# Two graph layers on one core: layer 1's norm statistics move to ScalarE, long tiles get a fifth pair of rows, four transposes move back, and the unused pass stores through SyncE

## The chip, the cores and the metric

The kernel runs on one core of a Trainium2 chip. The metric is the device time of one execution in microseconds (us); less is better. TensorE is called PE in the profile, VectorE is DVE, ScalarE is ACT, GpSimd is POOL and SyncE is SP. Every engine works through its own instructions in order and waits on semaphores for the others.

## The reference, cut to what matters

There are 3327 nodes with 512 features and one sparse adjacency matrix. Layer 0 is a graph attention layer, layer 1 a gated mix of attention and plain sum. Each is followed by a residual and a layer norm. Layer 1, which the change touches, is:

```python
def _L1_gnn_ref(x, adj_a, adj_b, W_sa, a_sa, W_gcnb, b_gcnb, Wa, ba, Wb, bb):
    attn_a = sigmoid(concatenate([adj_a @ x, x], axis=1) @ Wa.T + ba)
    attn_b = sigmoid(concatenate([adj_b @ x, x], axis=1) @ Wb.T + bb)
    h = x @ W_sa
    scores = (h @ a_sa[0, :Hd])[:, None] + (h @ a_sa[0, Hd:])[None, :]
    e = where(adj_a != 0, exp(-leaky_relu(scores, 0.01)), 0.0)
    x_a = (e / (sum(e, axis=1, keepdims=True) + 1e-05)) @ h
    x_b = adj_b @ (x @ W_gcnb) + b_gcnb
    return sigmoid(attn_a * x_a + attn_b * x_b)
x = _layernorm(x + _L1_gnn_ref(x, adj, adj, ...))     # both adjacencies are the same
```

The layer norm takes the mean and the variance of each node's 512 numbers. The inputs are about as sparse as 9 neighbours to a node.

## The kernel before

**Two passes.** `sparse_pass` does all the work as long as no node has more neighbours than its tables hold; it computes a flag for that. `dense_pass` stands in an `If` on the flag and isn't taken with these inputs. At the end of the program every engine loads the flag and takes the other side of the branch, whose few instructions bring the semaphores to the values that they would have after `dense_pass`.

**Nodes and tiles.** Nodes are sorted by their number of neighbours and cut into 26 tiles of 128. `CAPS` gives the number of neighbour rows of each tile, from 4 to 14. Two tiles of 14 have an extra "stair" row for the few nodes with still more. Rows are fetched from a table in memory by indirect DMAs that GpSimd issues (`gather`, L615), one DMA for a row of each of 128 nodes. They land in seven buffers of six rows, three tiles ahead of their use.

**Layer 1's loop.** The last loop runs over 26 tiles and three more turns to empty the pipeline. The order of tiles alternates long and short ones; the first five have 5, 6, 6, 6 and 7 rows and the last two 5 and 4. In turn i, tile j is summed, the next tile j1 gets its weights, the one before, jp, is projected, and jpp, two before, is finished. Order on each engine is the order of the calls, for the scheduler is off (`manual_schedule`). In short:

- ScalarE scales jp's plain sum (`sp`, L1027); TensorE turns `sw` and then `sp` of jp, four 128x128 transposes each (`turn`, L998), and ScalarE copies both out (`sT`, L1000).
- TensorE adds tile j's unpaired rows into `acc` (`plain_sum(j, False)`, L988).
- VectorE adds each row, weighted, into `sw` (`weighted`, L967), and adds pairs of rows in place (L969), so that TensorE sums one row for two. `paired` says which: four pairs a tile, five from 13 rows on.
- VectorE makes `za` of jpp from the projection (L1035) and ScalarE takes its tanh (L1037).
- TensorE projects jp's `sw` (`project`, `po<-wsa`, L1007), adds the sums of two (L988), and projects jp's `sp` (`po<-wg`, L1007). VectorE makes tile j1's weights in between (`weights_a`, L902 to L924).
- VectorE adds the residual to jpp's `za` (L1059), finishes j1's weights (`weights_b`, L929 to L932). ScalarE then starts the next weighted sum with the tile's own row (`scaled_first`, `sw`, L951). VectorE takes the statistics of `za` (`norm.add`: `bn_stats` L660 and `bn_aggr` L661). At the ends of eight groups of up to four tiles, 13 small instructions follow (`rsqrt`, L669 to L676).
- In the next turn ScalarE normalises the group's tiles (L1052) and GpSimd scatters them to the output (L145).

The next turn's `weighted` begins with `sw`, which ScalarE has just started (L951).

Of the kernel before, what the change touches and what calls it, by code (L numbers as in the profile page):

```python
# [8 lines left out]
F32 = mybir.dt.float32  # L9
AF = mybir.ActivationFunctionType  # L10
ALU = mybir.AluOpType
# [3 lines left out]
P = 128  # L15
LN_EPS = 1e-5
I32 = mybir.dt.int32
BF16 = mybir.dt.bfloat16
# [7 lines left out]
CAPS = (14, 12, 11, 10, 9, 9, 8, 8, 7, 6, 6, 5) + (14, 13, 11, 10, 10, 9, 9, 8, 8, 7, 7, 6, 5, 4)  # L26
# [10 lines left out]
GRP = 4  # L37
# [42 lines left out]
def sparse_pass(  # L80
# [39 lines left out]
    nc = tc.nc  # L120
    N, F = out.shape
# [33 lines left out]
    x1 = [x1a.tile([P, NG[0], ROW], F32, name="x1a"), None]  # L155
# [19 lines left out]
    def place(j):  # L175

        return (0, j) if j < NG[0] else (1, j - NG[0])
# [5 lines left out]
    def row1(j):  # L183
        g, i = place(j)
        return x1[g][:, i, :]
# [403 lines left out]
    m0 = ctx.enter_context(tc.tile_pool(name="m0", bufs=2))  # L589
# [89 lines left out]
    class Norm:  # L679
# [6 lines left out]
        def add(self, k, y):  # L686
# [8 lines left out]
            self.first, self.mv = k + 1, None  # L695
            return done


    first = list(range(NG[0]))

# [123 lines left out]
    norm = Norm(m0, "n0", {3, 7, 11, 15, 19, 22, 24, 25})  # L824
    weigh_a(order0[0])
    weigh_b(order0[0])
    ready = [[], []]
    for i in range(NT + 3):
        if i + AHEAD < NT:
            j = order0[i + AHEAD]  # L830
# [3 lines left out]
        ready = [ready[1], []]  # L834
# [4 lines left out]
        if 0 < i <= NT:  # L839
            j = order0[i - 1]  # L840
            y = row1(j)[:, 0:F]
# [3 lines left out]
            done = norm.add(i - 1, y)  # L845
# [24 lines left out]
    m1 = ctx.enter_context(tc.tile_pool(name="m1", bufs=2))  # L870
# [65 lines left out]

    def paired(j):

        left = 4 + (CAPS[j] >= 13)
        got_ = set()  # L940
        for s0, n, g, _ in got[j]:
            for i in range(0, n - 1, 2):
                if left:
                    got_.add(s0 + i)
                    left -= 1
        return got_

    def scaled_first(j):

        sw = sums[j] = m1.tile([P, F], F32, tag="sw", name=f"sw{j}")  # L950
        nc.scalar.activation(sw, row1(j)[:, 0:F], AF.Copy, scale=ew[j][:, 0:1])  # L951
        if j in T0:
            scaled = m1.tile([P, F], F32, tag="scaled", name=f"scaled{j}", bufs=1)
            nc.scalar.activation(scaled, stair[j][:, 0:F], AF.Copy, scale=ws2[j])
            stair_sum[j] = ps1.tile([P, F], F32, tag="stair", name=f"stair_sum{j}")
            nc.tensor.matmul(stair_sum[j], to_node, scaled, start=True, stop=True)

    def weighted(j, part):

        e, sw, two = ew[j], sums[j], paired(j)  # L960
        cut = max(two) + 2
        for s0, n, g, _ in got[j]:
            for i in range(n):
                s = s0 + i
                if (s < cut) != (part == 0):
                    continue
                nc.vector.scalar_tensor_tensor(sw, g[:, i, 0:F], e[:, s : s + 1], sw, ALU.mult, ALU.add)  # L967
                if s - 1 in two:
                    nc.vector.tensor_add(g[:, i, 0:F], g[:, i - 1, 0:F], g[:, i, 0:F])  # L969
        if part == 1 and j in T0:  # L970
            nc.vector.tensor_add(sw, stair_sum[j], sw)

    def plain_sum(j, sums_of_two):
        two = paired(j)
        single, double = [(ident, row1(j)[:, 0:F])], []
        for s0, n, g, _ in got[j]:
            for i in range(n):
                if s0 + i - 1 in two:
                    double.append((ident, g[:, i, 0:F]))
                elif s0 + i not in two:  # L980
                    single.append((ident, g[:, i, 0:F]))
        if j in T0:
            single.append((to_node, stair[j][:, 0:F]))
        if not sums_of_two:
            plain[j] = ps.tile([P, F], F32, tag="acc", name=f"acc1_{j}", bufs=2)
        rows = double if sums_of_two else single
        for i, (to, row) in enumerate(rows):
            nc.tensor.matmul(  # L988
                plain[j], to, row, start=(not sums_of_two and i == 0),
                stop=(sums_of_two and i == len(rows) - 1),  # L990
            )

    def turn(j, half):

        src = sums[j] if half == 0 else zs[j, "sp"]
        pt = (ps, ps1)[half].tile([P, KT, P], F32, tag="pt", name=f"pt{half}_{j}")
        for k in range(KT):
            nc.tensor.transpose(pt[:, k, :], src[:, k * P : (k + 1) * P], ident)  # L998
        sT = zs[j, half] = m1.tile([P, KT, P], F32, tag=f"sT{half}", name=f"sT{half}_{j}")
        nc.scalar.copy(sT, pt)  # L1000

    def project(j, half):
        sT, wt = zs[j, half], (wsa, wg)[half]
        if half == 0:
            proj[j] = ps1.tile([P, F], F32, tag="po", name=f"po{j}", bufs=2)
        for k in range(KT):
            nc.tensor.matmul(proj[j], sT[:, k, :], wt[:, k, :], start=(half + k == 0), stop=(half + k == KT))  # L1007

    ends = {3, 7, 11, 15, 19, 22, 24, 25}
    norm = Norm(m1, "n1", ends)  # L1010
    at_ = lambda i: order[i] if 0 <= i < NT else None
    for i in range(3):
        got[at_(i)] = gather(table1, at_(i))
# [1 line left out]
    weights_a(at_(0))  # L1015
    weights_b(at_(0))
    scaled_first(at_(0))
    ready = None
    for i in range(NT + 3):
        j, j1, jp, jpp = at_(i), at_(i + 1), at_(i - 1), at_(i - 2)  # L1020
        if at_(i + 3) is not None:
            got[at_(i + 3)] = gather(table1, at_(i + 3))
        if j1 is not None:
            own_score(j1)
        if jp is not None:
            sp = zs[jp, "sp"] = m1.tile([P, F], F32, tag="sp", name=f"sp{jp}")
            nc.scalar.activation(sp, plain[jp], AF.Copy, scale=gates[jp][:, 1:2])  # L1027
            turn(jp, 0)
            turn(jp, 1)
        if j is not None:  # L1030
            plain_sum(j, False)
            weighted(j, 0)
        if jpp is not None:
            za = zs[jpp] = m1.tile([P, F], F32, tag="za", name=f"za{jpp}", bufs=GRP + 3)
            nc.vector.scalar_tensor_tensor(za, bias_g, gates[jpp][:, 1:2], proj[jpp], ALU.mult, ALU.add)  # L1035

            nc.scalar.activation(za, za, AF.Tanh, scale=0.5)  # L1037
        if jp is not None:
            project(jp, 0)
        if j is not None:  # L1040
            plain_sum(j, True)
        if j1 is not None:
            weights_a(j1)
        if j is not None:
            weighted(j, 1)
        if jp is not None:
            project(jp, 1)
        if ready:
            k0, scale, shift = ready
            for k in range(k0, i - 2):  # L1050
                z = zs[order[k]]
                nc.scalar.activation(  # L1052
                    z, z, AF.Identity, scale=scale[:, k - k0 : k - k0 + 1], bias=shift[:, k - k0 : k - k0 + 1]
                )
                scatter("out", out, own(order[k]), z, N - 1)
            ready = None
        if jpp is not None:
            za = zs[jpp]
            nc.vector.scalar_tensor_tensor(za, za, 0.5, row1(jpp)[:, 0:F], ALU.mult, ALU.add)  # L1059
        if j1 is not None:  # L1060
            weights_b(j1)
            scaled_first(j1)
        if jpp is not None:
            ready = norm.add(i - 2, zs[jpp])


@with_exitstack
def dense_pass(
# [21 lines left out]
    nc = tc.nc  # L1090
    N, F = x.shape
    H, _, FO = W0.shape
# [45 lines left out]
    x1 = x1_pool.tile([P, NT, F], F32, name="x1")  # L1138
# [25 lines left out]
    with tc.tile_pool(name="feats", bufs=1) as feats_pool:  # L1164
# [3 lines left out]
        with tc.tile_pool(name="p0", bufs=1) as p0, tc.tile_pool(name="p0s", bufs=2) as p0s, tc.tile_pool(  # L1168
            name="p0ps", bufs=2, space=PSUM
# [15 lines left out]
            for c0 in range(0, N, CH):  # L1185
# [3 lines left out]
                for t in range(c0 // P, (c0 + cw + P - 1) // P):  # L1189
                    r, o = rows(t), t * P - c0  # L1190
# [45 lines left out]
        with tc.tile_pool(name="m0", bufs=2) as m0p, tc.tile_pool(name="m0o", bufs=1, space=PSUM) as pso, tc.tile_pool(  # L1236
            name="m0t", bufs=2, space=PSUM
        ) as pst:
            for n0 in range(0, N, NB):
                nw = min(NB, N - n0)  # L1240
                tiles = list(range(n0 // P, (n0 + nw + P - 1) // P))
                rr = m0p.tile([P, 2, H, NB], F32, tag="rr", name=f"rr{n0}")
                for j, t in enumerate(tiles):
                    r = rows(t)
# [7 lines left out]
                for t0, g in groups(G):  # L1252
# [4 lines left out]
                    for t in range(t0, t0 + g):  # L1257
                        r = rows(t)
# [30 lines left out]
                for j, t in enumerate(tiles):  # L1289
                    r = rows(t)  # L1290
# [9 lines left out]
                    y = x1[:r, t, :]  # L1300
# [21 lines left out]
    with tc.tile_pool(name="p1", bufs=1) as p1, tc.tile_pool(name="p1s", bufs=2) as p1s, tc.tile_pool(  # L1322
        name="p1ps", bufs=2, space=PSUM
# [18 lines left out]
        for t in range(NT):  # L1342
            r = rows(t)
# [24 lines left out]
    with tc.tile_pool(name="m1", bufs=2) as m1p, tc.tile_pool(name="m1o", bufs=1, space=PSUM) as pso, tc.tile_pool(  # L1368
        name="m1t", bufs=2, space=PSUM
    ) as pst:  # L1370
        for n0 in range(0, N, NB):
# [3 lines left out]
            for j, t in enumerate(tiles):  # L1375
                r = rows(t)
# [36 lines left out]
            for j, t in enumerate(tiles):  # L1413
                r = rows(t)
# [13 lines left out]
                za = m1p.tile([P, F], F32, tag="za", name=f"za{t}")  # L1428
# [5 lines left out]
                y = x1[:r, t, :]  # L1434
# [4 lines left out]
            normalise(m1p, f"b{n0}", tiles, stats)  # L1439
            for t in tiles:  # L1440
                r = rows(t)
                nc.gpsimd.dma_start(out[t * P : t * P + r, :], x1[:r, t, :])


def gat_then_gated_gnn(tc, x, xT, xB, xL, adj, adjT, adjB, adjL, diag, xo, W0, W0B, b0, a_self, a_neigh, *rest):
# [71 lines left out]
```

## Time and profile before

| | us |
|---|---|
| median of 3 runs | 974.06 (973.56 to 977.38) |
| profiled execution | 1108.9 |
| its span | 1107.2 |
| layer 1's loop in it, first gather wait to last scatter | about 659 to 1095 |
| PE, DVE, ACT, POOL busy in the span | 830.1, 716.9, 278.9, 623.3 |

The profiled execution took 134.8 us longer than the median, so durations in it show which engine waits for which, and a sum of differences is made in its microseconds. A row of the groups gives the line, the engine, the operation, output and input, the count, and then the busy time, the mean duration of one in ns and the idle time before it. A row of the timeline gives the start, the duration, and in brackets how long the engine had been idle and what ended that. Successive instructions overlap a little, so the distance from start to start is what an instruction costs its engine.

### The profile page before, as it was taken

To read this page: it belongs to the slowest core of one execution; us is meant where nothing else is said; L and a number is where in the kernel's file an instruction comes from. 1 tells how busy PE (TensorE), PEld (TensorE's weight loads), DVE (VectorE), ACT (ScalarE), POOL (GpSimd) and SP (SyncE) were. 2 spreads that over 40 slices of the span, in tenths; PEclk is the share of its full clock that TensorE was granted. 3 is DMA by queue.
4 is the path that set the end of the run, shared out by engine and by line. 5 is a ranking of instruction groups with operands and counts; after the bars stand their busy time and mean duration, and the time that the engine had idled before them with its cause. 6 is when DMAs were issued, how large, how long until landed. Compare 5 with 4: busy or idle time off the path is not lost.

```text
span 1107.2 us, 10091 instructions
## 1 busy us (share of the span) xinstructions
PE 830.1 (75%) x2534; PEld 435.9 (39%) x2534; DVE 716.9 (65%) x2118; ACT 278.9 (25%) x820; POOL 623.3 (56%) x664
## 2 busy tenths in 40 slices
PE   4499973028768697868848976689898989697992
PEld 3377751014334343434424432244344434343441
DVE  4286786187333673855536655398797989968872
ACT  1022120004221442433313421122222222131331
POOL 7410247607675466466766437737777777776311
PEclk9698995557778898989979985889898999898997
DMA  9899899603976567486766417726676576766200
GB/s 324 316 359 399 346 321 381 198 0 105 394 232 173 149 204 206 147 307 197 213 187 202 145 62 200 204 77 190 178 191 185 173 193 174 189 177 180 76 29 31
DMA packets 74243, 221.88 MB, mean 200 GB/s; under 512 B 14944, under 2 KB 19216, under 8 KB 73280
## 3 DMA queue, kind: packets, MB, share of 16 engines
q0 software_dynamic: 47008, 153.87, 47.1%
q1 hardware_dynamic: 24512, 65.17, 15.6%
q10 hardware_dynamic: 2656, 2.10, 0.6%
q8 instruction: 23, 0.38, 0.1%
q14 instruction: 44, 0.36, 0.1%
HBM read 200.01 MB, written 28.55 MB: 206 GB/s over the span
## 4 chain that ended last, share of the span: by engine, by line
PE 40%; issue 16%; POOL 12%; DVE 12%; another core or an unknown queue 9%; DMA 5%; ACT 5%; ACTq 0%; DVEq 0%; POOLq 0%; SPq 0%
PE acc L763 12%; PE pf L351 7%; POOL g L615 7%; PE po L1007 6%; PE acc L988 6%; PE pcol L787 2%; DMA g<-table,srt 2%; DMA at<-in_adjB 2%; PE acc L752 2%; DVE sw L967 2%; POOL out L145 1%; ACT g L758 1%; POOL lists L145 1%; PE pt L998 1%
## 5 line engine op out<-in xcount | busy, mean ns | idle before, releaser
L615 POOL DMA_INDIRECT g<-table,srt x464 | 476.1, 1026 | 217.9 <-issue 145.8
L763 PE MATMUL acc<-g,ident 128*128 128x512 f32 x504 | 238.3, 629 | 2.4 <-issue 2.4
L967 DVE SCALAR_TENSOR_TENSOR sw<-g,e,sw 128x512 f32<-128x512 f32 x226 | 169.4, 750 | 13.5 <-ACT sw L951 6.2
L763 PEld LDWEIGHTS acc<-g,ident 128*128 128x128 f32 x504 | 103.5, 206 | 139.8 <-issue 126.8
L988 PE MATMUL acc<-g,ident 128*128 128x512 f32 x262 | 126.4, 617 | 13.5 <-DMA g<-table,srt 9.5
L1007 PE MATMUL po<-wsa,sT 128*128 128x512 f32 x208 | 101.4, 633 | 18.3 <-issue 13.3
L351 PE MATMUL pf<-w,xc 128*128 128x260 f32 x416 | 103.4, 411 | 13.4 <-DVE w L291 13.4
L760 DVE TENSOR_TENSOR g<-g,w 128x512 f32<-128x512 f32 x176 | 109.7, 692 | 0.6
L351 PEld LDWEIGHTS pf<-w,xc 128*128 128x128 f32 x416 | 84.7, 206 | 29.4 <-DVE w L291 13.9
L1007 PE MATMUL po<-wg,sT 128*128 128x512 f32 x208 | 93.7, 593 | 0.0
L758 ACT ACTIVATE g<-g,w 128x128 f32<-128x128 f32 x304 | 91.9, 390 | 2.7 <-issue 2.2
L787 PE MATMUL pcol<-v,xt 128*128 128x8 f32 x208 | 35.7, 299 | 74.1 <-ACT xt L784 57.1
L988 PEld LDWEIGHTS acc<-g,ident 128*128 128x128 f32 x262 | 51.0, 197 | 82.6 <-issue 54.0
L1007 PEld LDWEIGHTS po<-wsa,sT 128*128 128x128 f32 x208 | 42.3, 206 | 77.3 <-issue 67.4
L969 DVE TENSOR_TENSOR g<-g 128x512 f32<-128x512 f32 x95 | 65.7, 692 | 3.3
L787 PEld LDWEIGHTS pcol<-v,xt 128*128 128x128 f32 x208 | 33.3, 244 | 80.6 <-ACT xt L784 62.0
L361 POOL DMA_DIRECT2D table<-row x26 | 14.4, 555 | 87.5 <-ACT st L360 87.5
L145 POOL DMA_INDIRECT out<-za,srt x26 | 28.8, 1108 | 57.2 <-ACT za L1052 51.1
L1007 PEld LDWEIGHTS po<-wg,sT 128*128 128x128 f32 x208 | 39.4, 190 | 48.8 <-issue 48.0
L1000 ACT COPY sT<-pt 128x512 f32<-128x512 f32 x52 | 29.1, 587 | 113.5 <-remote 56.7
L379 PE MATMUL pc<-at,pow 128*32 128x512 bf16 (+1 forms) x182 | 23.9, 434 | 36.7 <-DMA at<-in_adjB 20.2
L784 ACT COPY xt<-x1t 128x512 f32<-128x512 f32 x26 | 15.2, 584 | 141.0 <-PE x1t L780 74.9
(236 smaller groups left out, 934.3 us busy)
## 6 DMA issues: line engine op xcount, KB each, us to landing
at<-in_adjB SPq DMA_DIRECT2D x78, 512.0 KB
g<-table,srt POOLq DMA_INDIRECT x464
table<-row POOLq DMA_DIRECT2D x26, 260.0 KB
xc<-in_xB SPq DMA_DIRECT2D x6, 1024.0 KB
own<-in_xo SPq DMA_DIRECT2D x1, 3640.0 KB
own<-table SPq DMA_DIRECT2D x1, 3640.0 KB
at<-in_adjL SPq DMA_DIRECT2D x13, 256.0 KB
table<-x1a SPq DMA_DIRECT2D x12, 260.0 KB
```

The lines of the kernel that those rows point to most:

```text
L145: put = nc.gpsimd.indirect_dma_start(out=dst, out_offset=bass.IndirectOffsetOnAxis(ap=rows, axis=0), in_=src, in_offset=None, bounds_check ...
L351: nc.tensor.matmul(pf[:, hh, :HC], xc[:, k, o : o + P], w0[:, k, hh, :], start=(k == 0), stop=(k == KT - 1))
L615: nc.gpsimd.indirect_dma_start(out=buf[:, q - q0, :], out_offset=None, in_=table[:, :], in_offset=bass.IndirectOffsetOnAxis(ap=srt[g][:, i ...
L758: nc.scalar.activation(gv[:, h, :], gv[:, h, :], AF.Copy, scale=w[:, s, h : h + 1])
L760: nc.vector.tensor_tensor(gv, gv, w[:, s, :].rearrange("p (h o) -> p h o", o=1).to_broadcast([P, H, FO]), ALU.mult)
L763: nc.tensor.matmul(acc, ident, buf[:, o + s - s0, 0:F], start=False, stop=(s == CAPS[j] and j not in T0))
L787: nc.tensor.matmul(pcol, xt1[:, k, :], v1[:, k, :], start=(k == 0), stop=(k == KT - 1))
L967: nc.vector.scalar_tensor_tensor(sw, g[:, i, 0:F], e[:, s : s + 1], sw, ALU.mult, ALU.add)
L969: nc.vector.tensor_add(g[:, i, 0:F], g[:, i - 1, 0:F], g[:, i, 0:F])
L988: nc.tensor.matmul(plain[j], to, row, start=(not sums_of_two and i == 0), stop=(sums_of_two and i == len(rows) - 1),)
L1000: nc.scalar.copy(sT, pt)
L1007: nc.tensor.matmul(proj[j], sT[:, k, :], wt[:, k, :], start=(half + k == 0), stop=(half + k == KT))
```

## The change

Five edits, four of them in layer 1's loop:

1. `Norm` is replaced by `SquareNorm`. The sum of a node's 512 numbers comes with the residual, as the accumulator output of L1059's instruction. One VectorE instruction of 128x1 makes minus the mean of it. ScalarE then squares `za` less its mean and adds the squares up (`Square` with a bias and an accumulator output), behind the start of the next weighted sum (L951). `bn_stats` and `bn_aggr` go.
2. The 13 small instructions (`finish`, also 13) move from the end of a group's last turn to the next turn, behind `weighted(j, 0)`.
3. `paired` allows five pairs, six from 13 rows on. A tile's rows lie in buffers of at most six, and pairs don't cross them. In the built program five of the 26 tiles get one more pair: both of 14 rows, the one of 12, and both of 11. The other tiles have no further pair to give.
4. The transposes of `sp` (`turn(jp, 1)`) move behind `plain_sum(j, False)` on TensorE.
5. `dense_pass` stores by SyncE instead of GpSimd. That pass isn't taken. In the built program the side of the branch that is taken loses one GpSimd instruction, which raised eight semaphores by what the dense pass's GpSimd stores would have added, and with it the waits on those semaphores ahead of it.

```diff
+    class SquareNorm:
...
+        def add(self, k, y):
+
+            i = k - self.first
+            less_mean = self.of[:, 0, i : i + 1]
+            nc.vector.tensor_scalar(less_mean, less_mean, -1.0 / F, None, ALU.mult)
+            square = self.pool.tile([P, F], BF16, tag="square", name=f"square{self.tag}{k}", bufs=1)
+            nc.scalar.activation(square, y, AF.Square, bias=less_mean, accum_out=self.of[:, 1, i : i + 1])
+            return k in self.ends
...
     def paired(j):
 
-        left = 4 + (CAPS[j] >= 13)
+        left = 5 + (CAPS[j] >= 13)
...
-    norm = Norm(m1, "n1", ends)
+    norm = SquareNorm(m0, "n1", ends)
...
             turn(jp, 0)
+        if j is not None:
+            plain_sum(j, False)
+        if jp is not None:
             turn(jp, 1)
         if j is not None:
-            plain_sum(j, False)
             weighted(j, 0)
+        if full:
+            ready = norm.finish(i - 3)
...
-            nc.vector.scalar_tensor_tensor(za, za, 0.5, row1(jpp)[:, 0:F], ALU.mult, ALU.add)
+            nc.vector.scalar_tensor_tensor(
+                za, za, 0.5, row1(jpp)[:, 0:F], ALU.mult, ALU.add, accum_out=norm.total(i - 2)
+            )
...
-        if jpp is not None:
-            ready = norm.add(i - 2, zs[jpp])
+        full = jpp is not None and norm.add(i - 2, zs[jpp])
...
-                nc.gpsimd.dma_start(out[t * P : t * P + r, :], x1[:r, t, :])
+                nc.sync.dma_start(out[t * P : t * P + r, :], x1[:r, t, :])
```

More of the change, by code (lines that the diff above doesn't have):

```diff
@@ L696, in add, with __init__, total, finish @@
             return done
+    class SquareNorm:
+        def __init__(self, pool, tag, ends):
+            self.pool, self.tag, self.ends = pool, tag, ends
+            self.first, self.of = 0, None
+        def total(self, k):
+            if self.of is None:
+                self.of = self.pool.tile([P, 2, GRP], F32, tag="of", name=f"of{self.tag}{k}")
+            i = k - self.first
+            return self.of[:, 0, i : i + 1]
+        def add(self, k, y):
+            i = k - self.first
+            less_mean = self.of[:, 0, i : i + 1]
[3 more added lines that the diff above has]
+            return k in self.ends
+        def finish(self, k):
+            n = k - self.first + 1
+            tile_ = lambda t: self.pool.tile([P, GRP], F32, tag=t, name=f"{t}{self.tag}{k}")[:, :n]
+            v, r, t, d = (tile_(x) for x in ("rv", "rr", "rt", "rd"))
+            nc.vector.tensor_scalar(v, self.of[:, 1, :n], 1.0 / F, LN_EPS, ALU.mult, ALU.add)
+            nc.vector.tensor_scalar(t.bitcast(I32), v.bitcast(I32), 1, None, ALU.logical_shift_right)
+            nc.vector.tensor_scalar(r.bitcast(I32), t.bitcast(I32), -1.0, float(0x5F3759DF), ALU.mult, ALU.add)
+            for _ in range(3):
+                nc.vector.tensor_mul(t, r, r)
+                nc.vector.scalar_tensor_tensor(t, t, -0.5, v, ALU.mult, ALU.mult)
+                nc.vector.scalar_tensor_tensor(r, t, 1.5, r, ALU.add, ALU.mult)
+            nc.vector.tensor_mul(d, self.of[:, 0, :n], r)
+            done = (self.first, r, d)
+            self.first, self.of = k + 1, None
+            return done
     first = list(range(NG[0]))
@@ L1017, in sparse_pass @@
     scaled_first(at_(0))
-    ready = None
+    ready, full = None, False
     for i in range(NT + 3):
```

## The prediction, made before the changed kernel had run

> **What bounds the kernel now.** I first read the windows, to see which engines are full in layer 1. The columns are the stretch in us, its length, then busy us and count for PE, PEld, DVE, ACT and POOL, the granted clock, the DMA share and GB/s.
>
> ```profile
> 855.00:900.00 45.00, 43.95 (x120) 20.34 (x118) 42.48 (x101) 11.18 (x28) 33.66 (x32) 1.00 0.63 181
> 900.00:950.00 50.00, 45.76 (x123) 21.12 (x124) 46.03 (x97) 14.16 (x33) 37.77 (x35) 1.00 0.65 181
> 980.00:1010.00 30.00, 27.65 (x79) 12.95 (x77) 28.67 (x61) 6.47 (x17) 23.60 (x22) 1.00 0.66 190
> ```
>
> TensorE and VectorE are both above 90%. ScalarE is a quarter full. GpSimd's instructions stand 0.30 us apart, so its 33.66 us of 45 are 43 with the gaps: it keeps up, but only just. Which of the first two sets the pace must come from their waits. I then read the groups of the loop.
>
> ```profile
> L967 DVE SCALAR_TENSOR_TENSOR sw<-g,e,sw 128x512 f32<-128x512 f32 x226 | 169.4, 750 | 13.5 <-ACT sw L951 6.2 <-issue 2.6 <-DVE sw L967 0.6
> L969 DVE TENSOR_TENSOR g<-g 128x512 f32<-128x512 f32 x95 | 65.7, 692 | 3.3
> L660 DVE BATCH_NORM_STATS2 st<-za 128x6 f32<-128x512 f32 x26 | 17.9, 687 | 0.1
> L661 DVE BATCH_NORM_AGGREGATE mvn<-st 128x2 f32<-128x6 f32 x31 | 5.7, 182 | 1.1
> ```
>
> At first sight 26 x (0.687 + 0.182) = 22.6 us of VectorE work go. But L967 already waits 6.2 us for `sw` L951, so the third view is VectorE's timeline where one turn meets the next. First a late turn, with statistics in it:
>
> ```profile
> 879.95 0.52 DVE L932 TENSOR_SCALAR e<-e,gate 128x12 f32<-128x12 f32 x1
> 880.15 0.68 DVE L660 BATCH_NORM_STATS2 st<-za 128x6 f32<-128x512 f32 x1
> 880.87 0.18 DVE L661 BATCH_NORM_AGGREGATE mvn<-st 128x2 f32<-128x6 f32 x1
> 881.26 1.54 DVE L967 SCALAR_TENSOR_TENSOR sw<-g,e,sw 128x512 f32<-128x512 f32 x2 [0.20 <-issue]
> ```
>
> Then the loop's first turn, which has none, since no tile is finished yet:
>
> ```profile
> 672.36 0.29 DVE L932 TENSOR_SCALAR e<-e,gate 128x6 f32<-128x6 f32 x1
> 673.44 1.56 DVE L967 SCALAR_TENSOR_TENSOR sw<-g,e,sw 128x512 f32<-128x512 f32 x2 [0.79 <-issue]
> ```
>
> The distance from L932 to the first L967 is 1.31 us with statistics and 1.08 us without. ScalarE sets it: L932's result frees `sw` L951, which starts 0.33 to 0.55 us after L932's start and takes 0.72:
>
> ```profile
> 880.50 0.72 ACT L951 ACTIVATE sw<-x1b,e 128x512 f32<-128x512 f32 x1 [1.22 <-DVE e L932]
> ```
>
> 0.33 + 0.72 = 1.05 and 0.55 + 0.72 = 1.27, and L967 starts 0.04 later. All turns without group end or normalising show 1.08 to 1.35. So the statistics stand in a wait that VectorE has anyway.
>
> Last I read the end of the program by its lines (name, count, minimum/median/maximum ns, first and last start):
>
> ```profile
> L1450 POOLq INC_SWDGE_SEM  x1: 1916/1916/1916, 1097.3 to 1097.3; - x1
> L1514 POOLq DRAIN  x3: 46/103/7093, 1099.2 to 1106.9; - x3
> ```
>
> After the last scatter has landed, GpSimd raises semaphores for 1.92 us, then drains for 7.09 us, and the span ends at 1107.2. Nothing else runs there.
>
> **What the Trainium skill says.** "VectorE: DVE Perf Modes", section "Two Vector instructions with no wait between them": an operation that writes out its accumulator is two instructions, the main one and an accumulator read. No VectorE row here shows that; ScalarE's own read is a row of 188 ns (L909), costing it 0.10 us from start to start. "Vector Engine (DVE) Microarchitecture Reference", section "Points that are easy to get wrong": a `scalar_tensor_tensor` with two non-bf16 SBUF sources runs at half throughput. The trace disagrees without an accumulator (L1059, two sources, 686 ns; L660, one source, 687 ns). "ScalarE: Activation LUTs", section "What ACT_TABLE_LOAD costs": an ACTIVATE with a pointer operand takes 280 ns + 0.833 ns for each of N elements, so 707 ns for 512. L951 takes 721, so `Square` should take about 0.72.
>
> **Part by part, on VectorE's path.**
>
> - Statistics out, 128x1 multiplication in: the work shrinks by 22.6 - 26 x 0.15 = 18.7 us, the path by nothing. It is covered by the 1.08 to 1.31 us wait for L951. If L951 came at once, 0.7 us a tile would be gained; it doesn't.
> - Accumulator read behind L1059: unseen. Below, 0.06 us (two independent small instructions, L929 to L930); above, 0.20 (dependent ones, L673 to L674). I take 0.13. Statistics and a next tile's weights meet in 23 turns; five of them don't feel it, for there ScalarE normalises four tiles (2.91 us) ahead of L951 and sets the distance alone (2.80 us). 18 x 0.13 = 2.3 us (1.1 to 3.6).
> - The 13 small instructions take 2.54 us wherever they stand. In the group-end turns L932 to L967 is 3.60 to 3.68 us now; afterwards 1.08 to 1.31 plus 2.54, so 0 to 0.25 more: 6 turns, +0.8. They no longer hide the `sw` wait.
> - Five more pairs: L969 costs 0.61 us from start to start: +3.05 us.
>
> VectorE's sum is 2.3 + 0.8 + 3.05 = +6.2 us.
>
> **On TensorE's path.** A pair saves one summed row, two passes of 0.429 us = 0.858: 5 x 0.858 = -4.3 us. The moved transposes cost the same; they let single rows (0.86 us for the tile's own row at least) run while `sp` is late. TensorE waited for `sp` at 723 (3.04 us), 834 (3.21), 914 (2.32), 963 (6.99) and 1011 (3.22). At 963 and 1011 the next projection waited for ScalarE's copy as well, so nothing is gained there; at the others about 1 us each.
>
> **On ScalarE.** `Square` and its read add about 0.72 + 0.10 us to each turn, behind L951 and ahead of `sp`: 21 us, all idle time. What queues behind it are `sp` and the copies `sT`. In the turn shown `sp` would end at 882.8 instead of 881.9. TensorE turned `sw` at 882.45 and, having a row to add first, needs `sp` at 883.7: covered. That cover is gone where TensorE is less than about 1 us behind VectorE; there up to 0.9 us of TensorE's slack goes, and then the projection is late next. I count 0 (bounds 0 and +3).
>
> **On GpSimd and SP.** No gather or scatter is added. Buffers come free by the same additions and sums, at most 0.6 us later in five tiles; L615 waited for TensorE's sums only 27.9 us in 7 places, early ones mostly. SP has nothing in the loop, and its dense stores aren't run.
>
> **Who decides.** In most turns VectorE has no wait but that for `sw`, so its +6.2 counts. But in the two 14-row tiles VectorE waits for TensorE's small products (2.76 us before 773, 3.77 before 844), so up to there TensorE decides. From 782 to 844 two pairs are added: TensorE comes 1.7 us earlier, plus 1 for the transposes, and VectorE later by 2 x 0.61 + 3 x 0.13 + 0.1 = 1.7, which leaves 2.0 of its 3.77. Both meet about 2.0 us earlier than now. Before 773 only the transposes help, by about 0.9, and VectorE's 4 x 0.13 + 0.1 = 0.6 are absorbed. By the profile that makes 6.2 - 1.7 - 0.6 - 2.0 - 0.9 = +1.0 us. As runs without the profiler needn't have these waits, I take the middle of +1.0 and +6.2: **+3.6 us**.
>
> **At the ends.** The last tile's chain from L1059 to L669 is 1.67 us now. With 0.60 + 0.13 + 0.20 + 0.10 + 0.91 + 0.10 it is 2.04: +0.4. The semaphore instruction goes: -1.9, for certain, as nothing covers it. The drain behind it may shrink too: 0 to -7.1; I take 0, as the span shows no reason for it.
>
> Sum: +3.6 + 0.4 - 1.9 = **+2.1 us**, so 1108.9 becomes 1111.0, and the median 974.06 becomes about 976. The profiled execution is 13.8% above the median; I carry the difference over in microseconds, for it is made of counted instructions.
>
> **Rivals.**
>
> - *The drain goes with the semaphore instruction.* For: it follows directly and is the only one of 7 us. Against: it may have to wait out all earlier indirect DMAs. -7.1 more: 969 us.
> - *TensorE sets the pace.* For: it stands still nowhere between 855 and 899. Against: VectorE doesn't either, and TensorE lost over 30 us to waits from 735 to 1045. Then -4.3 + 0.4 - 1.9 = -5.8, and up to 3 more for the three waits for `sp`: 965 to 968 us.
> - *The accumulator output slows L1059 itself* (slower). If it streams at half pace, 512 elements cost 0.53 us more (0.686 less the 0.15 of a 128x1 operation), in 18 turns +9.5, giving 986 us. It decides, against my sum of +2.1 and the bound of 4.9 named below, from 2.8 / 18 = 0.16 us a turn on. For: the skill's sentence; against: L1059 isn't halved now. With it I count a `Square` that needs another function table: the page's one load took 1283 ns, and two a tile would be 67 us.
> - *The fifth pair hardly happens.* It does in 5 tiles of 26, as counted above.
>
> **How the numbers follow.** My sum: 0.57, range 971 to 982. The drain goes: 0.17. TensorE paces: 0.10. L1059 slows: 0.16. Half a per cent, 4.9 us, is about what a measurement can tell from no change. Faster by more: most of the drain and TensorE cases and 0.02 of mine, 0.21. Slower: the last case and 0.16 of mine, 0.32. Within: 0.47. The range, 966 to 987, takes in the drain's and TensorE's values and most of the slow case.
>
> **What would show it.** After: L967's wait for `sw` L951 grows from 6.2 to 15 to 25 us; the distance from L932 to L967 stays at 1.1 to 1.35; L969 counts 100; L988 loses ten instructions; `sp`'s transposes wait less than 14.0 us; INC_SWDGE_SEM is absent; DRAIN stays near 7 us. I am wrong if L932 to L967 falls below 0.9 us, if L1059 takes over 0.9 us, or if the drain shrinks.

## The result, and the profile after

The changed kernel takes **971.48 us** (median of 20 runs, 969.49 to 975.73) against 974.23 us (20 runs, 971.03 to 977.38) before: ratio 0.9974, 95% interval 0.9963 to 0.9985, so 2.75 us less. Predicted was 976, 2.1 us more. The time lies in the predicted range, which at 21 us was wide; the direction was wrong. The profiled execution of the changed kernel took 969.49 us with a span of 967.8 us, so it is an ordinary one.

One thing has to be known to read the numbers: on four of the six chips that the experiments ran on, and in the profiled execution before, every kernel took about 1100 us, with engines standing still for 5 to 20 us at a time in places where ordinary executions have no wait, so times from there scatter by 1%, their ratios are taken from the fast executions alone, and their traces serve for undisturbed turns and for the program's end.

**The groups of layer 1**, after. The lines are 40 to 45 higher than before (L951, L967, L969, L988 and L1059 have become L991, L1007, L1009, L1028 and L1103):

```profile
L1007 DVE SCALAR_TENSOR_TENSOR sw<-g,e,sw 128x512 f32<-128x512 f32 x226 | 169.4, 750 | 27.9 <-ACT sw L991 23.8
L1009 DVE TENSOR_TENSOR g<-g 128x512 f32<-128x512 f32 x100 | 69.2, 692 | 3.4
L1103 DVE SCALAR_TENSOR_TENSOR za<-za,x1b 128x512 f32<-128x512 f32 x14 | 9.6, 684 | 1.4 <-ACT za L1081 1.4
L716 DVE TENSOR_SCALAR ofn<-ofn 128x1 f32<-128x1 f32 x26 | 4.7, 181 | 0.1
L1103 DVE DVE_READ_ACCUMULATOR za<-za,x1b 128x1 f32 x14 | 1.1, 81 | 0.0
L718 ACT ACTIVATE squaren<-za,ofn 128x512 bf16<-128x512 f32 x26 | 18.4, 707 | 1.0 <-DVE ofn L716 1.0
```

The statistics are gone from VectorE, and L1007 now waits 23.8 us for ScalarE's `sw`, against 6.2 in the profile before (8.5 in an execution of ordinary length with layer 1 as before): the room that the statistics filled stands empty. The residual with its accumulator output takes 684 ns, as without (686), and the read behind it 81 ns. `Square` takes 707 ns.

**VectorE's timeline** where two turns meet (start, duration, in brackets the idle time before it and its end):

```profile
754.84 0.68 DVE L1103 SCALAR_TENSOR_TENSOR za<-za,x1a 128x512 f32<-128x512 f32 x1
755.45 0.08 DVE L1103 DVE_READ_ACCUMULATOR za<-za,x1a 128x1 f32 x1
755.45 0.15 DVE L969 TENSOR_SCALAR gate<-gate 128x1 f32<-128x1 f32 x1
755.52 0.16 DVE L970 TENSOR_SCALAR gate<-gate 128x2 f32<-128x2 f32 x1
755.64 0.16 DVE L971 RECIPROCAL gate<-gate 128x1 f32<-128x1 f32 x1
755.84 0.29 DVE L972 TENSOR_SCALAR e<-e,gate 128x12 f32<-128x12 f32 x1
756.04 0.15 DVE L716 TENSOR_SCALAR ofn<-ofn 128x1 f32<-128x1 f32 x1
756.92 1.54 DVE L1007 SCALAR_TENSOR_TENSOR sw<-g,e,sw 128x512 f32<-128x512 f32 x2 [0.73 <-ACT sw L991]
```

From L972 to L1007 it is 1.08 us, the shortest distance of the turns before. The accumulator read and L969 start at the same 755.45, 0.61 us behind the residual. Before, L929 started 0.60 behind it, so **the read costs nothing** here:

```profile
878.97 0.68 DVE L1059 SCALAR_TENSOR_TENSOR za<-za,x1a 128x512 f32<-128x512 f32 x1
879.57 0.15 DVE L929 TENSOR_SCALAR gate<-gate 128x1 f32<-128x1 f32 x1
```

**The windows** of the late loop (busy us and count for PE, PEld, DVE, ACT, POOL; clock, DMA share, GB/s):

```profile
800.00:840.00 40.00, 39.22 (x108) 18.03 (x108) 36.21 (x84) 12.63 (x33) 31.46 (x29) 1.00 0.67 188
840.00:880.00 40.00, 35.30 (x95) 15.73 (x95) 34.31 (x92) 14.93 (x36) 31.16 (x30) 1.00 0.69 194
```

GpSimd issues 29 or 30 instructions in each window of 40 us. With 0.30 us between them, 30 need 31.16 + 9 = 40.2 us: it never stops. From 600 to 900 us its list of waits has no stop longer than that gap:

```profile
POOL g L615 <- issue: 50.3, 165, 0.3
POOL g L615 <- DMA g<-table,srt: 4.9, 16, 0.3
POOL out L145 <- issue: 4.0, 13, 0.3
```

(Us in total, times, longest; the other lines of the list are short and none is longer than 0.3 either.) The profile before had shown it stopped 27.9 us for TensorE's sums; in an execution of ordinary length it isn't, with layer 1 as before either.

**The end of the program**, after: the last scatter, and the drain by its lines.

```profile
958.85 0.98 POOL L145 DMA_INDIRECT out<-za,srt  x1 [2.54 <-ACT za L1096]
L1559 POOLq DRAIN  x3: 50/109/7155, 959.8 to 967.5; - x3
```

INC_SWDGE_SEM is absent and the drain about as long as before, 7.16 us against 7.09. But it starts at 959.8, 0.9 us behind the start of the last scatter. Before, the drain started 5.4 us behind the last scatter, at 1099.2, because there is one more kind of instruction ahead of INC_SWDGE_SEM:

```profile
1093.87 0.99 POOL L145 DMA_INDIRECT out<-za,srt  x1 [2.07 <-ACT za L1052]
L1450 POOLq EVENT_SEMAPHORE  x5: 17/42/43, 1096.9 to 1097.2; - x5
```

GpSimd had waited until 1096.9 for the scatters to land: the last update of the last scatter's semaphore stands in that trace at 1096.74. This wait went with the instruction that it stood in front of. SyncE still waits for the landing (its first L1559 semaphore wait ends at 962.0, 3.1 us behind the scatter's start), while GpSimd drains. From the last scatter's start to the span's end it was 1107.2 - 1093.87 = 13.3 us and is 967.8 - 958.85 = 8.9: **4.4 us less**, and not 1.9. Every other trace agrees: 13.3 to 13.5 us with GpSimd's stores, 8.9 to 9.1 with SyncE's.

### The profile page after: what moved, and what is told of

The parts are those of the page before. It is cut to its first block, busy times and chain, and to the rows that moved or that the text cites. A ratio compares the mean times of both kernels' runs of the same rounds, so it can differ in the third digit from the quotient of the medians.

```text
span 967.8 us, 10126 instructions
## 1 busy us (share of the span) xinstructions
PE 795.7 (82%) x2524; PEld 416.1 (43%) x2524; DVE 702.6 (73%) x2123; ACT 296.9 (31%) x872; POOL 623.3 (64%) x664
## 4 chain that ended last, share of the span: by engine, by line
PE 40%; DVE 20%; DMA 14%; POOL 14%; issue 7%; ACT 5%; DVEq 0%; ACTq 0%; POOLq 0%
PE acc L803 17%; POOL g L615 10%; DMA g<-table,srt 10%; PE pf L351 8%; DVE sw L1007 6%; PE po L1047 4%; PE pcol L827 3%; PE acc L792 2%; DVE g L1009 2%; DMA at<-in_adjB 2%; PE acc L1028 2%; DVE ent L72 1%; ACT xt L824 1%; ACT za L1096 1%; DMA a_row<-in_a_self 1%
## 5 line engine op out<-in xcount | busy, mean ns | idle before, releaser
L803 PE MATMUL acc<-g,ident 128*128 128x512 f32 x504 | 227.6, 607 | 1.4 <-DVE g L800 1.4
L1007 DVE SCALAR_TENSOR_TENSOR sw<-g,e,sw 128x512 f32<-128x512 f32 x226 | 169.4, 750 | 27.9 <-ACT sw L991 23.8
L803 PEld LDWEIGHTS acc<-g,ident 128*128 128x128 f32 x504 | 99.4, 198 | 130.4 <-issue 99.7
L1028 PE MATMUL acc<-g,ident 128*128 128x512 f32 x252 | 123.2, 612 | 25.3 <-DVE g L1009 15.6
L351 PE MATMUL pf<-w,xc 128*128 128x260 f32 x416 | 104.3, 414 | 13.4 <-DVE w L291 13.4
L1047 PE MATMUL po<-wsa,sT 128*128 128x512 f32 x208 | 94.4, 597 | 0.2 <-ACT sT L1040 0.2
L1028 PEld LDWEIGHTS acc<-g,ident 128*128 128x128 f32 x252 | 46.8, 192 | 94.8 <-issue 41.3
L1009 DVE TENSOR_TENSOR g<-g 128x512 f32<-128x512 f32 x100 | 69.2, 692 | 3.4
L145 POOL DMA_INDIRECT out<-za,srt x26 | 28.7, 1105 | 54.2 <-ACT za L1096 48.1
L1081 ACT ACTIVATE za<-za 128x512 f32<-128x512 f32 x26 | 16.4, 630 | 151.8 <-DVE za L1079 151.8
L827 PE MATMUL pcol<-v,xt 128*128 128x8 f32 x208 | 31.7, 279 | 32.6 <-ACT xt L824 32.5
L1047 PEld LDWEIGHTS po<-wsa,sT 128*128 128x128 f32 x208 | 37.7, 191 | 38.2 <-issue 37.4
L770 ACT ACTIVATE w<-w 128x40 f32<-128x40 f32 (+10 forms) x26 | 6.1, 236 | 138.5 <-DVE w L769 138.4
L757 DVE TENSOR_TENSOR w<-g,srt 128x20 f32<-128x20 f32 (+3 forms) x55 | 9.5, 178 | 51.8 <-DMA g<-table,srt 51.1
## 6 DMA issues: line engine op xcount, KB each, us to landing
at<-in_adjL SPq DMA_DIRECT2D x13, 256.0 KB, 13.3
```

The lines of the kernel that those rows point to most:

```text
L145: put = nc.gpsimd.indirect_dma_start(out=dst, out_offset=bass.IndirectOffsetOnAxis(ap=rows, axis=0), in_=src, in_offset=None, bounds_check ...
L351: nc.tensor.matmul(pf[:, hh, :HC], xc[:, k, o : o + P], w0[:, k, hh, :], start=(k == 0), stop=(k == KT - 1))
L803: nc.tensor.matmul(acc, ident, buf[:, o + s - s0, 0:F], start=False, stop=(s == CAPS[j] and j not in T0))
L827: nc.tensor.matmul(pcol, xt1[:, k, :], v1[:, k, :], start=(k == 0), stop=(k == KT - 1))
L1028: nc.tensor.matmul(plain[j], to, row, start=(not sums_of_two and i == 0), stop=(sums_of_two and i == len(rows) - 1),)
```

## The experiments

### The stores alone

The kernel before with the fifth edit alone:

```diff
-                nc.gpsimd.dma_start(out[t * P : t * P + r, :], x1[:r, t, :])
+                nc.sync.dma_start(out[t * P : t * P + r, :], x1[:r, t, :])
```

> The kernel before with the fifth edit alone: dense_pass stores by SyncE. Layer 1 is untouched. Landing theory: in the profile before, GpSimd waited for the last scatter's landing, then raised semaphores for 1.92 us, then drained for 7.09 us; without the semaphore instruction the waits ahead of it go too and the drain starts at once behind the branch, while the scatter is still landing, so the time falls by the whole stretch, 12.3 us from the last scatter's end to the span's end less 8.0 in the profile after: -4.3 us. Instruction theory (the prediction's step): -1.9 us. Drain theory: the drain shrinks as well, -9 us. If the gain of the whole change lies in layer 1 instead: within 1 us of before.

> The fifth edit alone, once more for runs without long stalls. Landing theory -4.4 us, instruction theory -1.9. From its trace: the traces so far show that the accumulator read costs nothing (0.61 us from the residual to the next instruction with it, 0.60 without) and that the five turns with a further pair grow by 0.5 to 0.7 us each. Gather theory: in this kernel VectorE's waits for gathers in the turns up to the eleventh are together about 1 us longer than in the changed one, and from the eleventh turn on the changed kernel is 2.9 us longer. Even-loss theory: the whole 3.2 us of the pairs and 0.8 of the group ends shows in layer 1's length.

Three measurements at 1100 to 1120 us gave 0.9952 (0.9874 to 1.0029), 0.9891 (0.9803 to 0.9978) and 0.9873 (0.9584 to 1.0162), and one pair of single executions 1094.14 against 1094.78; they are too rough for 4 us. The one at 975 us decides: **970.15 against 975.01 us, ratio 0.9953 (0.9935 to 0.9972)**, 4.6 us less (2.7 to 6.3). The landing theory's 4.4 us lies inside; the instruction theory's ratio, 1 - 1.9/974 = 0.998, lies outside, as does the drain theory's 0.991. Its trace ends like this:

```profile
962.50 0.98 POOL L145 DMA_INDIRECT out<-za,srt  x1 [2.08 <-ACT za L1052]
L1514 POOLq DRAIN  x3: 50/109/7162, 963.4 to 971.2; - x3
```

0.9 us from scatter to drain and 8.9 to the end of the span (971.4), as in the changed kernel. So by its ratio the fifth edit alone gains more than all five together do: 0.9953 against 0.9974. The other four lose 0.0021 of 974 us, 2.0 us. The two intervals overlap a little, so the times alone say about 0 to 4.

This trace is also the only one of layer 1 as before that has no long stalls. Laid beside the changed kernel's, turn by turn from L932 (L972) to the next, with turns counted from 0 as `i` is in the loop, it shows where the others lose. Both are counted from their first L932 (L972): the code ahead of it, which the edits don't touch, took 6.35 us longer in this one execution.

| up to the end of turn | 4 | 6 | 10 | 11 | 13 | 15 | 20 | 24 | span's end |
|---|---|---|---|---|---|---|---|---|---|
| changed kernel later by, us | -0.45 | -0.39 | +0.08 | +0.82 | +1.22 | +1.69 | +2.60 | +2.30 | +2.70 |

Up to turn 10 next to nothing is lost, though turns 7 and 9 have a further pair each and grew by 0.52 and 0.38 us. In turns 4 and 10 VectorE waits for a gather, and what was lost before shortens that wait. In turn 10 it is the stair row of the next tile, of 14 rows. First a line of the list of VectorE's waits of the stores-only kernel, then the same line of the changed kernel's list:

```profile
DVE spread_l L636 <- DMA g<-table,ids: 1.0, 1, 1.0
```

```profile
DVE spread_l L636 <- DMA g<-table,ids: 0.6, 1, 0.6
```

So GpSimd, which never stops, sets the time of turn 10's end. Behind it no turn waits for a gather, and lengthenings add up.

### Layer 1 alone

The changed kernel with `dense_pass` storing by GpSimd as before:

```diff
-                nc.sync.dma_start(out[t * P : t * P + r, :], x1[:r, t, :])
+                nc.gpsimd.dma_start(out[t * P : t * P + r, :], x1[:r, t, :])
```

> The changed kernel with dense_pass storing by GpSimd as before, so the four edits in layer 1 alone. Landing theory: the tail keeps its 12.3 us, so the time is that of the changed kernel plus 4.3: about +1.5 us against before. Instruction theory with a gain in layer 1: -2.75 + 1.9 = -0.9 us. The prediction's own sum for these edits: +4.0 us (3.6 + 0.4). If TensorE paces layer 1: -4 to -7 us.

> The four edits in layer 1 without the fifth, once more. The runs of the first comparison took 1102 us for the kernel before, and engines stood still in them for up to 18 us at a time with nothing that the profile shows to wait for, so they separate no theory of 3 us. In runs near the 974 us of before, landing theory: -2.75 us for the whole change plus the 4.4 us that the tail measures (13.3 us from the last scatter's start to the span's end with GpSimd's stores, 8.9 with SyncE's) = +1.6 us. Instruction theory with a gain in layer 1: -0.9 us. The prediction's sum: +4.0 us.

At about 1105 us these gave 1.0121 (1.0064 to 1.0178) and then 0.9974 (0.9933 to 1.0015). The two contradict each other, and neither is used. The tail in the second one's trace is again 13.4 us (1097.77 to 1111.1), with the waits and INC_SWDGE_SEM back. The time of these four edits comes from the difference above and from the traces.

### The norm alone, and the pairs alone

The kernel before with `SquareNorm` and `finish` as in the change, everything else as before; and the kernel before with one number changed:

```diff
-        left = 4 + (CAPS[j] >= 13)
+        left = 5 + (CAPS[j] >= 13)
```

> The kernel before with the first two edits alone: SquareNorm and the 13 small instructions moved to the next turn. Four pairs, transposes and stores as before. Theory that VectorE paces and the statistics stood in its wait for sw: 18 accumulator reads of 0.11 to 0.13 us, +0.8 for the group ends, +0.4 for the last tile: +3.2 to +3.5 us. Theory that removing the statistics does save VectorE time: -5 us or more. Theory that TensorE paces: +0.4 us, the last tile's chain alone.

> The first two edits alone once more (SquareNorm, and the 13 small instructions in the next turn). Theory that VectorE paces everywhere: +3.2 to +3.5 us against before (18 accumulator reads of 0.11 to 0.13, 0.8 for group ends, 0.4 for the last tile). Gather theory (VectorE waits for GpSimd up to the eleventh turn, so only later turns count): 9 to 11 reads = 1.1 to 1.3, group ends 0.5, last tile 0.4: +2.0 us. Statistics worth something after all: below 0.

> The first two edits alone once more, four pairs, transposes and stores as before. The prediction's sum for them: 2.3 for reads, 0.8 for group ends, 0.4 for the last tile: +3.5 us. By the traces read since, the read costs 0.00 to 0.01 us and only group ends behind the eleventh turn count, 0.6, and the last tile 0.4: +1.0 us. In runs near 974 us the measurement tells these two apart at its edge; in its trace, turns with no group end are as long as before to 0.05 us by the second, and 0.13 longer by the first.

> The kernel before with the third edit alone: a fifth pair of rows (a sixth from 13 rows on), which adds five VectorE additions and takes five sums from TensorE. Theory that VectorE paces: up to 5 x 0.61 = +3.05 us, less where it waits for TensorE's small products in the two 14-row tiles, so +1 to +3 us. Theory that TensorE paces: 5 x 0.858 = -4.3 us. If both alternate: within 1 us of 0.

The norm gave 1.0049 (0.9962 to 1.0137), 0.9871 (0.9777 to 0.9965) and 1.0077 (1.0038 to 1.0116), the pairs 1.0033 (0.9973 to 1.0093), all at 1100 us and more: no verdict on the time in either case. But many turns take the same in every trace in which they have no stall, to about 0.02 us, except for a step of 0.2 to 0.3 us: ScalarE starts the next `sw` 0.33 us behind L932 (L972) in some, and 0.54 to 0.59 in others. So the shortest of each can be compared (us; six traces of layer 1 as before, three with the norm alone, one with the pairs alone, three of layer 1 as changed):

| turn (rows of its tile) | before | norm alone | pairs alone | changed |
|---|---|---|---|---|
| 3 (6) | 10.27 | 10.28 | 10.27 | 10.28 |
| 16 (8) | 12.45 | 12.47 | 12.46 | 12.46 |
| 20 (9) | 13.24 | 13.25 | 13.25 | 13.25 |
| 23 (9) | 14.72 | 14.72 | 14.73 | 14.72 |
| 7 (14, further pair) | 19.50 | 19.50 | 20.03 | 20.02 |
| 9 (12, further pair) | 15.48 | 15.75 | 16.12 | 16.13 |
| 11 (14, further pair) | 20.33 | 20.33 | 20.69 | 20.70 |
| 13 (11, further pair) | 14.68 | 14.96 | 15.34 | 15.34 |

Turns with statistics and read but neither pair nor group end (the first four rows) are equal to 0.02 us: the norm costs nothing in them, and the 0.13 us a turn that the prediction charged isn't there. In turns 9 and 13 the norm alone shows the step in all of its three traces, the kernel before in two and three of its six and the changed kernel not in its shortest; whether the norm makes it likelier is not shown. A further pair costs 0.36 to 0.66 us.

### One statistic a group

The kernel before with the statistics of the last tile of each group alone, used for the whole group. It leaves out 18 of the 26 statistics, so its output isn't the layer norm's:

```diff
+    class LastNorm(Norm):
+        def add(self, k, y):
+            if k not in self.ends:
+                return None
+            self.mv = self.pool.tile([P, GRP, 2], F32, tag="mv", name=f"mv{self.tag}{k}")
+            stats(self.pool, y, self.mv[:, 0, :])
...
-    norm = Norm(m1, "n1", ends)
+    norm = LastNorm(m1, "n1", ends)
```

> The kernel before with bn_stats and bn_aggr for the last tile of each group only, and its scale and shift used for the whole group; 18 of 26 statistics, 18 x 0.87 = 15.7 us of VectorE work, are left out with nothing in their place. Theory that they stand in the wait for ScalarE's sw: within 1.5 us of before, and L932 to L967 stays at 1.08 us or more in the turns without them. Theory that VectorE's work as such paces: -8 to -15 us.

> 18 of the 26 statistics left out, as before, one look at the turns without long stalls. Theory that statistics stand in the wait for sw: L932 to L967 stays at 1.08 us or more in turns without them, and turns behind the eleventh are as long as with the statistics, to 0.2 us. Theory that VectorE's work as such paces: 0.7 to 0.87 us less in each such turn.

The ratio was 0.9955 (0.9895 to 1.0016) at about 1100 us, and one pair of single executions took 1101.94 against 1094.78: undecided in time. The turns decide. VectorE's timeline of the single execution, where two turns meet without statistics:

```profile
928.14 0.29 DVE L932 TENSOR_SCALAR e<-e,gate 128x9 f32<-128x9 f32 x1
929.22 1.54 DVE L967 SCALAR_TENSOR_TENSOR sw<-g,e,sw 128x512 f32<-128x512 f32 x2 [0.79 <-ACT sw L951]
```

With statistics these two lines stood 1.08 to 1.35 us apart, and without them they do so too, 1.08 here. In all 26 turns none is below 1.08. The turns of 8 and 9 rows of the table above (16, 20 and 23) take 12.45, 13.24 and 14.72 us with 18 statistics left out: what they took before. Only turns 11 and 19 are shorter by more than 0.1 us (0.17 and 0.14). So the **statistics stood in the wait for `sw`**; this is shown, not only argued.

### The residual put into the wait

If that room is empty now, something can be put into it. The changed kernel with the next tile's weights ahead of the residual:

```diff
+        if j1 is not None:
+            weights_b(j1)
+            scaled_first(j1)
         if jpp is not None:
             za = zs[jpp]
             nc.vector.scalar_tensor_tensor(
                 za, za, 0.5, row1(jpp)[:, 0:F], ALU.mult, ALU.add, accum_out=norm.total(i - 2)
             )
-        if j1 is not None:
-            weights_b(j1)
-            scaled_first(j1)
```

> The changed kernel with one reordering: weights_b(j1) and scaled_first(j1) go ahead of the residual of jpp. ScalarE starts the next weighted sum's sw about 0.73 us earlier against VectorE, and VectorE does the residual, the accumulator read and the 128x1 multiplication (0.60 + 0.11 + 0.19 us) inside the 1.08 us between L972 and the next L1007. Theory that VectorE paces and waits there for sw: about 0.73 us for each of 23 turns, less the 4 turns in which ScalarE normalises a group there, so -14 to -17 us against the changed kernel, and -17 to -20 against before. Theory that TensorE paces: within 1 us of the changed kernel. If both are near the limit, TensorE takes over after some turns: -5 us.

> The same reordering once more (weights_b and scaled_first ahead of the residual), since the first comparison ran at 1104 us for the kernel before, with stalls of several us in every execution. In runs near 974 us: theory that VectorE paces and waits for sw, about 0.7 us for each of some 20 turns: -12 to -15 us against the changed kernel, -15 to -18 against before. TensorE paces: about -3 against before, like the changed kernel. TensorE takes over in part: -5 to -10 against before.

The first, at 1104 us, gave 0.9905 (0.9854 to 0.9955). The second: **969.68 against 974.54, ratio 0.9946 (0.9931 to 0.9961)**, 5.3 us less than before and 2.7 less than the changed kernel (0.9946 against 0.9974). By its size this is the third theory's, that TensorE takes over in part; the trace shows another cause. The residual does stand in the room from L972 on:

```profile
758.69 0.38 DVE L972 TENSOR_SCALAR e<-e,gate 128x12 f32<-128x12 f32 x1
758.89 0.69 DVE L1106 SCALAR_TENSOR_TENSOR za<-za,x1a 128x512 f32<-128x512 f32 x1
759.50 0.08 DVE L1106 DVE_READ_ACCUMULATOR za<-za,x1a 128x1 f32 x1
759.62 0.15 DVE L716 TENSOR_SCALAR ofn<-ofn 128x1 f32<-128x1 f32 x1
759.86 1.57 DVE L1007 SCALAR_TENSOR_TENSOR sw<-g,e,sw 128x512 f32<-128x512 f32 x2
```

Most turns without a wait for a gather became 0.3 to 0.8 us shorter. But in turn 10 VectorE came earlier to the stair row and waited 3.4 us for it instead of 0.6, and all that the turns before had won was gone. Only the turns behind it brought a gain.

### Normalising behind the next weights

The same, with ScalarE's normalising of a group moved as well:

```diff
-        if ready:
-            k0, scale, shift = ready
...
         full = jpp is not None and norm.add(i - 2, zs[jpp])
+        if ready:
+            k0, scale, shift = ready
...
```

> The changed kernel with weights_b and scaled_first ahead of the residual, and with ScalarE's normalising of a group (L1096) behind both. In the reordered kernel VectorE still waited 2.1 us for sw in the turns that normalise four tiles (turns 15, 19 and 23 behind the last wait for a gather). Theory that VectorE paces behind the eleventh turn: 3 x 2.1 = 6 us less than with the reordering alone, which was 4.9 below before: -11 us against before. If sp or the copies sT, which now come 2.9 us later in these turns, hold TensorE up: -3 to -6. If GpSimd's later scatters hold up gathers: no gain over the reordering, -5.

> The changed kernel with weights_b and scaled_first ahead of the residual and the group's normalising behind both, once more. In runs near 974 us: -11 us against before if VectorE paces behind the eleventh turn; -3 to -6 if sp or sT, 2.9 us later in these turns, hold TensorE up; -5 if GpSimd's later scatters hold up gathers.

The first, at 1110 us: 0.9879 (0.9779 to 0.9978). The second: **965.60 us (8 runs) against 975.01 (27), ratio 0.9908 (0.9884 to 0.9932)**, 9.0 us less than before. It beats both kernels. VectorE's waits, from 570 us on:

```profile
DVE spread_l L636 <- DMA g<-table,ids: 3.6, 1, 3.6
...
DVE sw L1007 <- ACT sw L991: 3.0, 6, 0.8
DVE gate L969 <- ACT e L949: 2.0, 3, 1.7
```

The wait for `sw` shrank from 23.8 to 3.0 us. Turns 15, 19 and 23, ahead of which a group was normalised in the changed kernel, became 2.31, 2.17 and 1.97 us shorter than there (its longest wait for `sw` was 2.4), so a wait taken away behind turn 10 is worth about its length. In turn 10 the wait for the stair row is 3.6 us, so what earlier turns won is lost here too: from the first L932 or L972 to turn 10's end it is 150.0 us with the stores alone, 150.0 in the changed kernel, 150.8 with the residual in the wait and 149.9 here. Some is given back at the end, where L969 waits 1.7 us for ScalarE's exponential, which stands behind the normalising.

> The last reordering (weights_b and scaled_first ahead of the residual, a group's normalising behind both), with four pairs a tile as before instead of five. VectorE paces behind the eleventh turn, and the further pairs of the tiles of 14, 11 and 11 rows lengthened their turns by 0.74, 0.39 and 0.55 us: 1.7 us less than with five pairs, so 0.9 % (9.0 us) below before becomes 10.7 us. If TensorE has become the bound there, each pair is worth 0.858 us the other way: 2 to 2.6 us more than with five, -6.5 against before.

With `left = 4` in that kernel: 1112.13 against 1117.46 us, 0.9976 (0.9944 to 1.0007), again at about 1100 us. Whether four pairs are better than five there stays open.

## Why the prediction was wrong, point by point

- **The statistics are worth nothing on the path**: right. Shown by the kernel with one statistic a group. L967's wait for `sw` grew from 6.2 to 23.8 us (15 to 25 was said), and the distance from L972 to L1007 stayed at 1.08 to 1.34 in turns in which ScalarE doesn't normalise.
- **The accumulator read, 18 x 0.13 = +2.3 us**: wrong. It starts together with the next instruction; 0.01 us a turn. The Trainium skill ("VectorE: DVE Perf Modes", "Two Vector instructions with no wait between them") says that there is a second instruction, and the trace agrees: 26 rows DVE_READ_ACCUMULATOR of 81 ns. Its duration isn't its price. I bounded it by other pairs of small instructions, and the lower bound, 0.06, should have been 0.
- **Five pairs, +3.05**: about right in the turns (0.36 to 0.66 each), but two of them are taken up by turn 10's wait. By the same two traces, the changed kernel's and the one with the stores alone, the three turns with a pair behind it grew by 0.74 + 0.39 + 0.55 = 1.7.
- **Group ends, +0.8**: not seen. As turns are counted here, from L932 (L972) to the next, the 13 small instructions behind turn 10 stand in turns 14, 18 and 22 in both kernels, and there the two traces differ by -0.08, +0.21 and -0.12 us, 0.0 in sum. They drift apart by 2.30 - 0.08 = 2.2 us behind turn 10, and the 0.5 of it that lies outside the three turns with a pair comes from turns 16, 17, 20 and 21 (+0.25, +0.18, +0.26, -0.17). There one trace has the step in `sw`'s start and the other hasn't. Layer 1 as before has it too: its six traces give 12.45 to 12.72 us for turn 16.
- **Who decides**: wrong in its engine. I asked TensorE or VectorE, and set GpSimd aside with "it keeps up, but only just", since the profile showed it waiting for TensorE. That was so in an execution of 1108.9 us. In those of 970 GpSimd never stops for another engine from 600 to 900 us, and its gathers set turn 10's end. My value by the profile, +1.0, was too low and the +3.6 that I took for caution too high: the traces say +1.7 for the pairs behind turn 10, and +2.2 with the steps of these two executions.
- **The last tile's chain, +0.4**: right, 2.70 - 2.30 = 0.4.
- **"The semaphore instruction goes: -1.9, for certain"**: this is the step that turned the sign: with -4.4 in its place the prediction's own sum is -0.4. The instruction is 1.92 us, but GpSimd waited for the scatters' landing only on its account. Without it the 7.1 us of the drain run while the last scatter lands. The term is -4.4 us by the traces and -4.6 by the time of the stores alone. The view shown in the prediction began at 1097.3, with the instruction; one that began at the last scatter's start, 1093.87, would have held the missing 2.5 us, and the text on the change even said that the waits go. The drain I bounded from 0 to -7.1; that it could start earlier at its full length I did not see.
- **The rivals.** The drain doesn't shrink: 7.16 us. TensorE doesn't pace: it waits for VectorE's pair sums (15.6 us in 18 places). The residual (L1059, now L1103) isn't slowed, 684 ns, and the whole program has one table load of 1283 ns, so `Square` brought none.
- **The transposes of `sp`**: were to wait less than 14.0 us, and do, 13.7 us in 10 places at TensorE's weight loads. But with the stores alone, where layer 1 is as before, it is 4.5 us in 5: the 14.0 came from the long execution, and between ordinary ones the waits grew. No cost of theirs is seen in the turns, but what the move is worth was not tried alone.

The sum in place of the predicted +2.1: pairs 1.7, last tile 0.4, tail -4.4, together -2.3 us. Measured are -2.75 (-1.5 to -3.6). Of the difference, 2.1 - (-2.3) = 4.4 us, 2.5 are the tail's (-1.9 said) and 1.9 layer 1's (+4.0 said, 2.1 seen); about 0.5 is left unexplained, and lies inside the interval.

## What to carry to other kernels

An instruction that goes takes with it the waits that stood ahead of it: price the stretch from the last work that remains to the end, not the instruction. Before asking which of two full engines paces a loop, find the waits for the producer (here GpSimd's gathers): gains and losses ahead of the last such wait vanished in it here, and only those behind it counted. Work taken out of a wait is worth nothing until something else is put into it.

## What the runs showed of the hardware that I had not expected

- VectorE's accumulator read costs no time when a small independent instruction follows: 0.61 us from the residual to the next instruction with it, 0.60 without. Where the next one needs the residual's result it is 0.73 us in both: to L716 in the kernel with the residual in the wait (758.89 to 759.62, with the read), and to the last tile's statistics before (1088.58 to 1089.30, without).
- GpSimd's drain at the end takes 7.1 us whether the last scatter has landed (7093 ns, started 5.4 us behind the scatter's start) or not (7155 and 7162 ns, started 0.9 behind it).
